# Reordering the steps of a bidirectional WKV kernel: r products two chunks ahead, an inverse ahead of a sigmoid, and a new order for a layer's first step

## The chip, the cores and the metric

The kernel runs on one core of a Trainium2 chip. The metric is device time in microseconds (us) of one execution, the median of three. Engines are named as the profile names them: PE is TensorE (matrix products), DVE is VectorE, ACT is ScalarE, POOL is GpSimd, SP is SyncE, which here only issues DMAs. Everything is in 32-bit floats.

## The reference

The input is `x`, 16 images of 192 channels and 56 x 56 = 3136 pixels. Three layers of the following kind are applied one after the other, and then one graph convolution. `_gn` is a group norm over 32 groups of channels.

```
# a WKV layer: x = x + layer(_gn(x)); t runs over the 3136 pixels
k, v, r = xs @ Wk.T, xs @ Wv.T, xs @ Wr.T
# forward: p, q are decayed sums of exp(k)*v and of exp(k)
y_t  = (p + e^(u+k_t) v_t) / (q + e^(u+k_t))      # then p, q take in pixel t
x_bi = 0.5 * (y of the pixels in order + y of the pixels in reverse)
h    = sigmoid(r) * x_bi
h    = (h - mean) * rsqrt(var + 1e-5)              # over the 192 channels
out  = h @ Wo.T
# the last layer: x + gelu(BN(concat(x, max of rolled differences) @ W + b))
```

## The kernel before

Two images make a pair, laid out as 128 partitions x 3 blocks x pixels (block 0: 128 channels of the first image, block 2: of the second, block 1: the remaining 64 of each). The 3136 pixels are cut into 7 chunks of 448. There are 8 pairs, and each goes through 3 WKV layers and the convolution; one pair in one layer is a *run*, so there are 32 runs. A WKV run has a forward pass over chunks 0 to 6 (functions `a_...`) and then a backward pass over chunks 6 to 0 (functions `b_...`). The sums are prefix scans on DVE (`scan`, L875).

Two streams of pairs are interleaved. While one run goes backward, a run of the other stream goes forward; I call these seven chunks a *turn*. The list of steps is worked out on the host in front of the launch. Turn by turn it has one backward chunk alone (`backward_alone`, chunk 6), then six steps in which a backward chunk and a forward chunk share the engines, then forward chunks alone. There are 24 turns. In 17 of them the forward run is a WKV run: their first shared step (backward chunk 5, forward chunk 0) is written in `both_a_first`, the five others (backward chunks 4 to 0) in `both_a`. In the other 7 the forward run is a convolution (`both_c`).

The order on each engine is written out by hand: the block runs under a manual schedule, so each engine executes its instructions in the order of the calls, and waits in that order. PE, DVE, ACT, POOL and SP each have a queue of their own. PSUM banks (7 of them) and SBUF slots (33) are handed out from lists in the order of the calls.

The work of one shared step, with the names used below:

- **r** (`b_gate`, L598 to L607): the product for the sigmoid, 14 matmuls. `b_exp` (L996) on ACT makes exp(-r) of it, `b_sigmoid` (L1003, L978) ln(1+...) and exp(-...).
- **k** and **v** (`a_keys`, `a_values`): the products of the forward chunk; `a_exp` (L920) on ACT, `a_ekv` (L940) on DVE.
- **scans** `b_q`, `b_p`, `a_q`, `a_p` (L875, DVE) and the **bonus** terms `b_den`, `b_num`, `a_den`, `a_num` (L890, DVE).
- **the inverses** of the denominators, on ACT as ln (L975) and exp(-...) (L978): of `b_den` for the mixing, of `a_den` for the forward output `a_y` (L982, POOL).
- **mixing** (`b_mix`, POOL, L1031, L1032, L1033 for each block): numerator x inverse, + forward output, x sigmoid.
- **the norm over channels**: `b_squares` (L1040, ACT); `b_sums` (L1047, L1049, PE) makes the sums **st**; `b_rs1` (L1055, ACT) squares the means; `b_rs2` (L1059, PE) subtracts them, called **rs2** below; `b_rs3` (L1063, L1065, ACT) makes the reciprocal deviation by ln and exp; `b_spread` (L1071, PE) spreads it over the partitions, **rsb**; `b_scale` (L1076, DVE) multiplies; `b_out` (PE, **ops**) is the product with Wo; `b_x` (L1089, DVE) adds it to x and stores x to DRAM.
- **count**: in a part of the steps ACT also takes two statistics (L734, L735) of a block of the next pair's input, twice per step.

In `both_a` the norm of a chunk is finished one step late: step *c* makes st of chunk *c* at its end, and rs2, rsb and ops of chunk *c* stand in the step after it. In `both_a_first` chunk 6's whole norm is done, and the sums of chunk 5.

`gap(...)` takes the next part of the coming run's group norm: sums, variance, `norm_fold` (POOL or DVE make the factor, L777 to L780, and ACT multiplies it into the weights of k and v, L770), and the weights of r.

On PE a `both_a` step has this order before: r of the next chunk, rs2, v, rsb, ops, k, st. On ACT: exp(-r), count, a save of the scan's edge, rs3, the sigmoid, the inverse for the mixing (blocks 0 and 2, then 1), the statistics of a stored chunk, squares and exps of k, rs1, and the inverse for y.

Of the kernel before, what the change touches and what calls it, by code (L numbers as in the profile page):

```python
# [55 lines left out]
NL = T // L  # L56
# [417 lines left out]
def fast_path(ctx: ExitStack, tc: tile.TileContext, flag, x, wproj, wfold, wcfold, wconst, wgroup, sums, picks, vecs, out):  # L474
# [499 lines left out]
    def ln(s, js=slice(0, 3)):  # L974
        S.activation(s.t[:, js, :], s.t[:, js, :], AF.Ln)  # L975
# [8 lines left out]


    def b_gate(run, c):
        product(run, "r", run.w[2], run.xb[c], c == NL - 1)

    def b_exp(run, c):
        if c == NL - 1:  # L990
# [328 lines left out]
    def count(z, most=1):  # L1319
        for _ in range(min(most, len(z))):  # L1320
            z_stats(*z.pop(0))

    def both_a(b, a, nback, nfront, z, loads):

        den = lambda: a[0].den[a[1]]
        l = of_stage(0.5)
        load_ahead(nback)
        store()
        if nback is not None:
            b_gate(*nback[1:])  # L1330
            b_exp(*nback[1:])
        count(z)
        b_q(*b)
        if l:
            b_rs2(*l)
            b_rs3(*l)
        b_sigmoid(*b)
        a_values(*a)
        if l:
            b_spread(*l)  # L1340
        b_p(*b)
        b_den(*b)
        for js in (AC, slice(1, 2)):
            ln(b[0].ek[b[1]], js)
            exp_minus(b[0].ek[b[1]], js)
        b_num(*b)
        b_mix(*b)
# [12 lines left out]
        b_squares(*b, (0,))  # L1360
        a_save(*a)
        count(z)
        exp_keys(nfront, (0, 2))
        b_squares(*b, (2,))
        exp_keys(nfront, (1,))
        b_squares(*b, (1,))
        b_sums(*b)
        a_p(*a)
        gap()
        a_den(*a)  # L1370
        b_rs1(*b)
        late[b] = 0.5
        invert(den())
        gap()
        a_num(*a)
        a_y(*a)
        gap()

    def both_a_first(b, a, nback, nfront, loads):

        den = lambda: a[0].den[a[1]]
        l = of_stage(0)
        load_ahead(nback)
        store()
        a_values(*a)
        b_squares(*l, (0, 2))
        b_q(*b)
        b_sigmoid(*b)
        b_p(*b)
        b_den(*b)  # L1390
        invert(b[0].ek[b[1]])
        b_num(*b)
        b_mix(*b)
        for u in loads:
            load_ahead(u)
        a_ekv(*a)
        b_squares(*l, (1,))
        if nback is not None:
            b_gate(*nback[1:])
        b_sums(*l)  # L1400
        b_rs1(*l)
        if nback is not None:
            b_exp(*nback[1:])
        a_q(*a)
        b_rs2(*l)
        b_rs3(*l)
        keys(nfront)
        a_p(*a)
        spread_and_scale(l)
        b_squares(*b, (0,))  # L1410
        a_save(*a)
        exp_keys(nfront)
        b_squares(*b, (2, 1))
        b_sums(*b)
        a_den(*a)
        b_rs1(*b)
        late[b] = 0.5
        invert(den())
        a_num(*a)
        add(l)  # L1420
        a_y(*a)

# [244 lines left out]
    def backward_alone(b, nback, nfront):  # L1667
        load_ahead(nback)
        load_ahead(nfront)
        store()  # L1670
        sum_up()
        b_q(*b)
        gap()
        b_den(*b)
        gap()
        invert(b[0].ek[b[1]])
        b_sigmoid(*b)
        b_p(*b)
        gap(G)
        b_num(*b)  # L1680
        b_mix(*b)
        for u in list(late):
            finish(u)
        if nback is not None:
            b_gate(*nback[1:])
            b_exp(*nback[1:])
        keys(nfront)
        exp_keys(nfront)
        late[b] = 0
# [13 lines left out]
    with tc.manual_schedule(engines={PE.engine, V.engine, S.engine, G.engine, nc.sync.engine}):  # L1703
        S.preload_act_table_set(TABLES)
        first = chains[0][0]
        for c in range(NL):
            load_ahead(("Z", first, c))
        for c in range(NL):
            count([(first, c, j) for j in ORDER], 3)
        for i, (b, f, z) in enumerate(steps):  # L1710
            nback, nfront, _ = steps[i + 1] if i + 1 < len(steps) else (None, None, None)
            for run in starts.get(i, ()):
                begin_later(run)
            if i == 0:
                keys(f)
                exp_keys(f)
            ahead = [("Z", run, c) for run, c, _ in (z if not b else [])]
            ahead += [nfront] if b and f else []
            ahead += [("Z", run, c) for run, c, _ in (steps[i + 1][2] if i + 1 < len(steps) else [])]
            ahead += [steps[i + 2][0]] if i + 2 < len(steps) else []  # L1720

            nkeys = nfront if nfront is not None and nfront[0] == "A" else None
            if f and not b and nkeys is None and nfront is not None and i + 2 < len(steps):
                far = steps[i + 2]
                if far[0] is None and far[1] is not None and far[1][0] == "A" and far[1][1] is f[1]:
                    nkeys = far[1]
            if f and nback is None and nfront is not None:
                near = [u for _, u, _ in steps[i + 1 : i + 4] if u is not None and u[0] == "A"]
                if len(near) > 1 and near[1][1] is near[0][1]:
                    ahead.append(near[1])  # L1730
            if not (b and f):
                for u in ahead:
                    load_ahead(u)
            if b and f and f[0] == "A":
                if of_stage(0) is None:
                    both_a(b[1:], f[1:], nback, nfront, z, ahead)
                else:
                    both_a_first(b[1:], f[1:], nback, nfront, ahead)
            elif b and f:
                both_c(b[1:], f[1:], nback, nfront, ahead)  # L1740
            elif f and f[0] == "A":
                forward_a(f[1:], nback, nfront, nkeys, z)
            elif f:
                forward_c(f[1:], nback, nfront)
            elif b:
                backward_alone(b[1:], nback, nfront)
            else:
                neither(nback, nfront)
            assert not z
        store()  # L1750
        assert not late and not unsummed and not convs and not half
# [100 lines left out]
```

## Time and profile before

| | us |
|---|---|
| median of 3 executions (lowest, highest) | 5217.34 (5207.30, 5221.48) |
| the profiled execution: its own time | 5220.16 |
| its span from first to last instruction | 5218.2 |
| PE busy | 4733.3 (91%) |
| DVE busy | 4750.5 (91%) |
| ACT busy | 3684.6 (71%) |
| POOL busy | 2889.2 (55%) |

A line of the profile names an engine, a line of the kernel, and output and inputs by the program's names. Times in timelines are us from the start of the span. PEclk is the share of its full clock that TensorE was granted. Busy time says how long an engine had something in hand; since two engines are at 91%, what matters is where each of them stands idle and for whom.

### The profile page before, as it was taken

Reading aid. Unit: us, or ns where it says so; the run is one execution under the profiler, and the core shown is the slowest. Engines: PE = TensorE matmul, PEld = TensorE weight load, DVE = VectorE, ACT = ScalarE, POOL = GpSimd, SP = SyncE. Lnnn points to the kernel's source line nnn. Section 1 sums busy time; section 2 is a strip of 40 time slices with the busy share of each in tenths; the row PEclk is TensorE's granted clock in tenths of the full one; section 3 lists DMA queues with packets and bytes.
Section 4 is the critical chain, followed back from the end, with each engine's and each line's share of the span. In section 5 each row is a group of like instructions: output and inputs, shape, how many; then the busy total and the mean of one; then the engine's idle time right before and its main releaser. Section 6 shows DMA issues by size and latency. Waiting matters only on the chain. (4 is left out here: it accounts for less than half of the span.)

```text
span 5218.2 us, 51856 instructions
## 1 busy us (share of the span) xinstructions
PE 4733.3 (91%) x15542; PEld 1498.8 (29%) x15542; DVE 4750.5 (91%) x6271; ACT 3684.6 (71%) x7163; POOL 2889.2 (55%) x2251
## 2 busy tenths in 40 slices
PE   7899998989899999998989999999898999999897
PEld 3222222223232222222323222222232322222222
DVE  6999999998989999999898999999889899999995
ACT  6777787776566777787656678777756667777772
POOL 1665665554545656565454556556545455666562
PEclk8999999999899999999989999999998999999998
DMA  5222222233232222223233223222333322222233
GB/s 154 69 82 87 90 86 89 85 110 97 90 116 72 87 90 93 82 90 122 93 93 101 84 75 100 88 85 87 128 93 101 93 74 77 72 84 77 80 104 120
DMA packets 314274, 482.47 MB, mean 92 GB/s; under 512 B 66432, under 2 KB 306688, under 8 KB 313984
## 3 DMA queue, kind: packets, MB, share of 16 engines
q1 hardware_dynamic: 312832, 477.59, 28.5%
q8 instruction: 126, 2.06, 0.2%
q10 hardware_dynamic: 1152, 1.48, 0.1%
q14 instruction: 164, 1.34, 0.1%
HBM read 324.83 MB, written 154.14 MB: 92 GB/s over the span
## 5 line engine op out<-in xcount | busy, mean ns | idle before, releaser
L875 DVE TENSOR_TENSOR_SCAN q<-fdecays,ek 128x449 f32<-128x449 f32 (+1 forms) x1008 | 1023.4, 1068 | 28.0 <-ACT ek L920 25.4
L875 DVE TENSOR_TENSOR_SCAN p<-fdecays,ekv 128x449 f32<-128x449 f32 (+1 forms) x1008 | 1020.3, 1065 | 0.6
L982 POOL TENSOR_TENSOR p<-p,q 128x1344 f32<-128x1344 f32 x168 | 512.0, 3047 | 830.3 <-ACT q L978 546.9
L1031 POOL TENSOR_TENSOR ekv<-ekv,ek 128x448 f32<-128x448 f32 x504 | 602.7, 1196 | 456.1 <-ACT ek L978 385.3
L1033 POOL TENSOR_TENSOR p<-p,sg 128x448 f32<-128x448 f32 x504 | 638.0, 1266 | 57.2 <-ACT ek L884 12.7
L1032 POOL TENSOR_TENSOR p<-p,ekv 128x448 f32<-128x448 f32 x504 | 606.1, 1203 | 39.5
L1040 ACT ACTIVATE ek<-p 128x448 f32<-128x448 f32 x504 | 286.4, 572 | 309.4 <-POOL p L1033 308.9
L886 POOL COPY ekv<-p 128x3 f32<-128x3 f32 x282 | 233.1, 827 | 488.0 <-DVE p L875 457.2
L1076 DVE TENSOR_TENSOR p<-p,rsb 128x448 f32<-128x448 f32 x504 | 282.4, 613 | 194.5 <-PE rsb L1071 194.4
L920 ACT ACTIVATE ek<-k,k 128x448 f32<-128x448 f32 x504 | 297.2, 632 | 225.3 <-PE k L601 179.2
L735 ACT ACTIVATE fjunk<-x 128x448 f32<-128x448 f32 x672 | 387.7, 577 | 40.1 <-DVE x L1089 13.4
L1071 PE MATMUL rsb<-rs,fpicks 32*128 32x448 f32 (+1 forms) x1008 | 359.2, 629 | 42.4 <-ACT rs L1065 42.4
L1159 POOL TENSOR_TENSOR ml<-ml,x 128x1344 f32<-128x1344 f32 x56 | 178.9, 3194 | 391.8 <-ACT ml L1150 391.8
L890 DVE SCALAR_TENSOR_TENSOR ek<-ek,fcc,q 128x896 f32<-128x896 f32 x336 | 379.1, 1167 | 0.0
L890 DVE SCALAR_TENSOR_TENSOR q<-ek,fcc,q 128x896 f32<-128x896 f32 x336 | 359.2, 1109 | 6.3 <-ACT cvb L954 4.6
L1089 DVE SCALAR_TENSOR_TENSOR x<-ops,fwob,x 128x448 f32<-128x448 f32 x504 | 314.2, 670 | 46.7 <-PE ops L601 26.6
L734 ACT ACTIVATE fjunk<-x 128x448 f32<-128x448 f32 x600 | 342.5, 571 | 11.4
L996 ACT ACTIVATE sg<-r,r 128x448 f32<-128x448 f32 x504 | 313.0, 627 | 33.5 <-PE r L607 20.7
L890 DVE SCALAR_TENSOR_TENSOR ekv<-ekv,fcc,p 128x896 f32<-128x896 f32 x336 | 330.1, 1022 | 0.0
L940 DVE SCALAR_TENSOR_TENSOR ekv<-v,v,ek 128x448 f32<-128x448 f32 x504 | 312.5, 672 | 16.6 <-PE v L601 8.0
L975 ACT ACTIVATE q<-q 128x1344 f32<-128x1344 f32 x168 | 221.5, 1318 | 125.5 <-DVE q L890 101.3
L890 DVE SCALAR_TENSOR_TENSOR p<-ekv,fcc,p 128x896 f32<-128x896 f32 x336 | 295.3, 919 | 6.5 <-POOL ekv L886 1.7
(235 smaller groups left out, 11546.4 us busy)
## 6 DMA issues: line engine op xcount, KB each, us to landing
x<-xd SPq DMA_DIRECT2D x240, 672.0 KB, 5.3
xd<-x SPq DMA_DIRECT2D x168, 672.0 KB, 3.9
x<-in_x_dram SPq DMA_DIRECT2D x320, 224.0 KB, 4.3
x<-in_x_dram SPq DMA_DIRECT2D x320, 112.0 KB, 4.2
out_dram<-ml SPq DMA_DIRECT2D x112, 224.0 KB, 2.3
m<-xd SPq DMA_DIRECT2D x112, 168.0 KB, 5.1
wkv<-in_wfold_dram SPq DMA_DIRECT2D x24, 640.0 KB, 5.6
out_dram<-ml SPq DMA_DIRECT2D x112, 112.0 KB, 2.3
```

The lines of the kernel that those rows point to most:

```text
L734: S.activation(junk, xt[:, j, :], AF.Identity, accum_out=stats[:, 0, j, c : c + 1])
L735: S.activation(junk, xt[:, j, :], AF.Square, accum_out=stats[:, 1, j, c : c + 1])
L875: V.tensor_tensor_scan(out, dec[:, column(j)].to_broadcast([P, L if first else L + 1]), e, 0.0, ALU.mult, ALU.add)
L890: by_channel(lambda js, i: V.scalar_tensor_tensor(dst.t[:, js, :], e.t[:, js, :], cc[:, i : i + 1], state.t[:, js, :], ALU.mult, ALU.add))
L940: V.scalar_tensor_tensor(e.t[:, j, :], ps[j][:, 0:L], b[:, j, :], run.ek[c].t[:, j, :], ALU.add, ALU.mult)
L982: G.tensor_mul(run.h[c].t, run.h[c].t, den.t)
L996: S.activation(sg.t[:, j, :], ps[j][:, 0:L], AF.Exp, bias=b[:, j, :], scale=-1.0, accum_out=run.chk[:, at : at + 1])
L1031: G.tensor_mul(y.t[:, j, :], y.t[:, j, :], den.t[:, j, :])
L1032: G.tensor_add(h.t[:, j, :], h.t[:, j, :], y.t[:, j, :])
L1033: G.tensor_mul(h.t[:, j, :], h.t[:, j, :], sg.t[:, j, :])
L1071: PE.matmul(ps[j][:, :L], pick[rows, j, :], rs[rows, :], start=True, stop=True)
L1089: V.scalar_tensor_tensor(xj, ps[j][:, 0:L], wob[:, column(j)], xj, ALU.add, ALU.add, accum_out=run.new[:, 0, j, c : c + 1] if c == 0 else ...
```

## The change

Five things are moved; nothing is computed in another way.

1. In `both_a`, r is made two chunks ahead: the product for backward chunk *c*-2 stands in step *c*, between the last squares and the sums. The call at the start of a step is kept, and `once` makes it do nothing where r was made before. So step 4 makes r of chunks 3 and 2, step 3 that of 1, step 2 that of 0, and steps 1 and 0 none.
2. In `both_a`, v stands ahead of rs2, and rs3 ahead of the count. PE's order becomes v, rs2, rsb, ops, k, r, st.
3. In `both_a`, the inverse for y stands ahead of rs1 on ACT; the inverse for the mixing's blocks 0 and 2 stands ahead of the sigmoid, that of block 1 behind it.
4. In `both_a_first`, the forward scan of q, the save and the product with exp(k) stand ahead of the backward bonus; chunk 6's rsb and ops stand ahead of k; the sigmoid stays ahead of the inverse, chunk 6's rs1 stands behind that inverse, and the inverse for y is taken ahead of the squares of chunk 5.
5. In `backward_alone`, the part of the next run's norm stands ahead of the sigmoid and of `b_p`.

```diff
     def b_gate(run, c):
-        product(run, "r", run.w[2], run.xb[c], c == NL - 1)
+        if once(run, "r", c):
+            product(run, "r", run.w[2], run.xb[c], c == NL - 1)
...
     def both_a(b, a, nback, nfront, z, loads, far):
         if nback is not None:
             b_gate(*nback[1:])
             b_exp(*nback[1:])
-        count(z)
-        b_q(*b)
+        a_values(*a)
         if l:
             b_rs2(*l)
             b_rs3(*l)
-        b_sigmoid(*b)
-        a_values(*a)
+        count(z)
+        b_q(*b)
         if l:
             b_spread(*l)
         b_p(*b)
         b_den(*b)
-        for js in (AC, slice(1, 2)):
-            ln(b[0].ek[b[1]], js)
-            exp_minus(b[0].ek[b[1]], js)
+        ln(b[0].ek[b[1]], AC)
+        exp_minus(b[0].ek[b[1]], AC)
+        b_sigmoid(*b)
+        ln(b[0].ek[b[1]], slice(1, 2))
+        exp_minus(b[0].ek[b[1]], slice(1, 2))
...
         b_squares(*b, (1,))
+        if far:
+            b_gate(*far[1:])
         b_sums(*b)
         a_p(*a)
         gap()
         a_den(*a)
+        invert(den())
         b_rs1(*b)
         late[b] = 0.5
-        invert(den())
...
     def both_a_first(b, a, nback, nfront, loads):
         b_p(*b)
+        a_q(*a)
+        a_save(*a)
+        a_ekv(*a)
+        b_squares(*l, (1,))
         b_den(*b)
         invert(b[0].ek[b[1]])
         b_num(*b)
         b_mix(*b)
...
-        a_ekv(*a)
-        b_squares(*l, (1,))
         if nback is not None:
             b_gate(*nback[1:])
         b_sums(*l)
         b_rs1(*l)
+        b_rs2(*l)
+        b_rs3(*l)
         if nback is not None:
             b_exp(*nback[1:])
-        a_q(*a)
-        b_rs2(*l)
-        b_rs3(*l)
+        a_p(*a)
+        a_den(*a)
+        invert(den())
+        spread_and_scale(l)
         keys(nfront)
-        a_p(*a)
-        spread_and_scale(l)
         b_squares(*b, (0,))
-        a_save(*a)
         exp_keys(nfront)
         b_squares(*b, (2, 1))
         b_sums(*b)
-        a_den(*a)
+        a_num(*a)
         b_rs1(*b)
         late[b] = 0.5
-        invert(den())
-        a_num(*a)
...
     def backward_alone(b, nback, nfront):
         invert(b[0].ek[b[1]])
+        gap(G)
         b_sigmoid(*b)
         b_p(*b)
-        gap(G)
...
+            far = steps[i + 2][0] if nback is not None and i + 2 < len(steps) else None
+            if far is not None and far[1] is not nback[1]:
+                far = None
```

More of the change, by code (lines that the diff above doesn't have):

```diff
@@ L1321, in count, with both_a @@
             z_stats(*z.pop(0))
-    def both_a(b, a, nback, nfront, z, loads):
+    def both_a(b, a, nback, nfront, z, loads, far):
         den = lambda: a[0].den[a[1]]
@@ L1723, in fast_path @@
             if f and not b and nkeys is None and nfront is not None and i + 2 < len(steps):
-                far = steps[i + 2]
-                if far[0] is None and far[1] is not None and far[1][0] == "A" and far[1][1] is f[1]:
-                    nkeys = far[1]
+                then = steps[i + 2]
+                if then[0] is None and then[1] is not None and then[1][0] == "A" and then[1][1] is f[1]:
+                    nkeys = then[1]
             if f and nback is None and nfront is not None:
@@ L1733, in fast_path @@
                     load_ahead(u)
+            far = steps[i + 2][0] if nback is not None and i + 2 < len(steps) else None
+            if far is not None and far[1] is not nback[1]:
+                far = None
             if b and f and f[0] == "A":
                 if of_stage(0) is None:
-                    both_a(b[1:], f[1:], nback, nfront, z, ahead)
+                    both_a(b[1:], f[1:], nback, nfront, z, ahead, far)
                 else:
```

## The prediction

> **What bounds the kernel now.** First the page's busy times, which name two engines at once:
>
> ```profile
> PE 4733.3 (91%) x15542; PEld 1498.8 (29%) x15542; DVE 4750.5 (91%) x6271; ACT 3684.6 (71%) x7163; POOL 2889.2 (55%) x2251
> ```
>
> So an average decides nothing, and I cut windows one `both_a` step long: two of a turn without counts, two of a turn with them (columns: stretch, length, then busy time of PE, its weight loads, DVE, ACT, POOL, and the granted clock).
>
> ```profile
> 409.10:432.70 23.60, 23.26 (x80) 7.12 (x80) 23.60 (x30) 19.25 (x38) 15.32 (x12) 1.00 0.28 89
> 432.70:456.20 23.50, 23.26 (x80) 7.12 (x80) 23.50 (x30) 19.24 (x37) 15.29 (x12) 1.00 0.26 87
> 1888.40:1915.50 27.10, 25.03 (x80) 7.64 (x80) 25.00 (x30) 21.58 (x45) 15.65 (x13) 0.94 0.22 76
> 1915.50:1942.70 27.20, 25.13 (x80) 7.65 (x80) 25.00 (x30) 21.59 (x45) 15.65 (x13) 0.94 0.30 97
> ```
>
> Without counts the step is 23.56 us and DVE never rests; PE lacks 0.3 us. With counts it is 27.2 us, nobody is full, and the clock falls below 1. Going through the starts of rsb turn by turn, 8 of the 17 turns are of the first kind, 9 of the second; three intervals of each turn (rsb of chunk 5 to 4, 3, 2) hold an r and are meant below.
>
> The waits say what the counted step hangs on:
>
> ```profile
> PEld st L1049 <- POOL p L1033: 191.9, 90, 4.1
> PE st L1049 <- POOL p L1033: 119.7, 90, 3.3
> ```
>
> PE idles 2.09 us for the mixing's end; then a half-clock spell; then r, exp(-r), the count, rs3, the sigmoid and the inverse stand in one row on ACT before POOL can mix again.
>
> The third reading is what surrounds rs2 on PE. In a counted step now, and then in a place where rs2 is followed at once by rsb:
>
> ```profile
> 1895.87 0.96 PE L1059 MATMUL st<-rs,fpicks 64*64 64x448 f32 x2
> 1896.76 1.02 PE L598 MATMUL v<-x,wkv 128*128 128x448 f32 x2
> ...
> 1901.27 1.97 PE L1071 MATMUL rsb<-rs,fpicks 32*128 32x448 f32 x6
> ```
>
> ```profile
> 1531.25 0.96 PE L1059 MATMUL st<-rs,fpicks 64*64 64x448 f32 x2
> 1533.54 3.55 PE L1071 MATMUL rsb<-rs,fpicks 32*128 32x448 f32 x6 [1.32 <-ACT rs L1065]
> 1537.01 1.86 PE L598 MATMUL v<-x,wkv 128*128 128x448 f32 x2
> ```
>
> ```profile
> 1530.30:1533.70 3.40, 2.08 (x9) 0.55 (x10) 3.40 (x10) 2.39 (x5) 0.53 (x1) 1.00 0.88 307
> 1533.70:1537.10 3.40, 3.40 (x7) 0.82 (x7) 3.33 (x6) 3.24 (x11) 0.00 (x0) 0.50 0.83 263
> 1537.10:1540.50 3.40, 3.40 (x6) 1.29 (x8) 3.40 (x6) 0.58 (x2) 0.00 (x0) 0.50 0.12 38
> 1540.50:1543.90 3.40, 3.40 (x12) 1.17 (x13) 3.12 (x4) 0.21 (x1) 0.00 (x0) 1.00 0.00 0
> ```
>
> Where v lies between them, ACT's ln and exp of rs3 (0.63 + 0.57 us) are hidden. Where it does not, PE idles 1.32 us and the clock then falls to half: rsb takes 3.55 instead of 1.97. This kernel has 23 places with a full product, rs2, 1.32 us and rsb at full clock, and all 23 are followed by a half-clock spell within 3.1 us. In 17 of the 23 the spell lasts 6.83 us, in the other six 3.41; in six of the 17 PE had a product ready right behind rsb.
>
> **What the Trainium skill says.** "TensorE: Matmul & The Clock Gate", Part 1: the clock goes to half or full by PE's activity in free-running windows of about 3.4 us. The trace agrees (spells of 3.41 or 6.83 us at 0.50), but the page warns of idle gaps above about 3.4 us, and here 1.32 us is enough: rs2 and rsb fill only part of the array. The measurement decides. The same page, Part 2, says that PE pulls only weight loads ahead, while matmuls keep their order; so nothing behind rsb can fill that gap. "SBUF — State Buffer", Who interferes with whom: a DVE instruction with two SBUF inputs and a GpSimd one that reads SBUF lock each other out. The trace agrees: bonus L890 on q takes 2.59 us instead of 1.71 where it meets mixing, and L1033 2.05 instead of 1.15.
>
> **The change, part by part.** Durations on PE, start to start: a product 4.51, st 1.64, rs2 0.89, rsb 1.90. Sums are made against the span, 5218.2; the profiled execution took 5220.2, 0.05% above the median of 5217.3.
>
> *`both_a`, v ahead of rs2, r ahead of st.* PE's loop becomes v, rs2, gap, rsb, ops, k, r, st = 4 x 4.51 + 0.89 + 1.90 + 1.64 = 22.5, with the gap (1.32, and 0.07 of lost overlap) 23.9; I take 24.05, since 23.57 minus the 0.31 idle and the 0.6 of slow st, plus 1.39, gives that. What else could bind, from rs2's end: ACT has rs3 1.25, count 1.33, save 0.2, inverse of two blocks 1.9, sigmoid 2.65, inverse of block 1 1.15, statistics 4.2, then 5.0 of squares, exps, save and count, which puts the last square's end at 17.7; half of st, v and rs2 behind it end at 24.0, as PE's own loop does. ACT's total, 21.6, has room, and the 2.65 of the inverse for y now ahead of rs1 is covered by v. DVE needs 23.55, with counts and some 1.3 us of locking 24.8. r's input: SP issued the load at 1874.26, it landed at 1878.79, and PE reaches r about 1885; r's banks come free with the x addition 8.2 us behind `b_scale`, about 10.6 on this scale, r starts at 12.3. So both are hidden, by 6 and 1.7 us. SP's own order of loads and stores is the same in both kernels.
>
> The gap throttles. By the window's phase I take no spell in 0.1 of the steps, one window (half of 3.41 = 1.7 lost) in 0.25, two (3.4) in 0.65: 2.6 us. The trace bounds this from 0 to 3.4, at six of its places two windows despite a ready product. Interval: 24.05 + 2.6 = 26.65. Against 27.2 with counts: -0.55 x 27 = -15. Against 23.56 without: +3.1 x 24 = +74. The interval from chunk 2 to 1 and the last one hold no r; DVE sets them (19.8 + 25.2 to 26.5, or 24.8 + 20.8 to 21.1: both 45 to 46), DVE's order there is unchanged: 0. The mixing's inverse ahead of the sigmoid starts POOL up to 2.65 earlier in the counted step; this is inside the loop, since PE ends it.
>
> *`both_a_first` and `backward_alone`, on PE from r of chunk 5 (511.5 in the turn at 500) to rsb of chunk 5 (553.5).* Now PE idles there 2.75 (k waits for L770) and 0.65. The fold ahead of the sigmoid takes away 2.7, since POOL's factor can be ready at 509.9 and ACT's inverse ends at 510.9. Added: (a) rs1 of chunk 6 now stands behind the inverse of chunk 5. On DVE `b_q`, `b_p` end at 518.8, `a_q` 521.8, exp(k)v 523.9, `b_den` 525.5; inverse to 528.2, rs1 528.7; PE ended st at 526.75: 2.0 idle in place of 0.65. (b) rs2 directly ahead of rsb: 1.3. (c) k now comes last, so st of chunk 5 waits for exp of k's block 1 and two squares behind it: 1.2. (d) rs2, gap, rsb in the first `both_a`: 1.3. Sum -2.7 + 1.35 + 1.3 + 1.2 + 1.3 = +2.4; a and c could be nothing and a shorter wait elsewhere could take 0.5 more: from 0 to 3. The two gaps of (a) and (b) throttle too: +2.6 (0 to 3.4; the gap of (d) is counted with the interval behind it). 5.0 x 17 = +85. Locking of `b_den` with chunk 6's mixing (3.15 instead of 1.72) goes, but DVE then only waits for rsb.
>
> *Convolution turns.* Only `backward_alone` acts: mixing of chunk 6 begins 2 us sooner; DVE waits 1.0 us for its end in L1125. -1.0 x 7 = -7 (0 to -14).
>
> Sum: -15 + 74 + 85 - 7 = +137, 5355; I state 5350.
>
> **The rivals.**
>
> *One window per gap* (spells end as soon as ops runs): loss 1.7, interval 25.75: -1.45 x 27 + 2.19 x 24 + 4.1 x 17 - 7 = +76, 5294. For it: six of the 23 spells last 3.41. Against: these begin a full us after rsb's end, and the six with a product ready all lasted 6.83.
>
> *Faster: no throttling.* r in PE's idle time keeps each window busy enough. Then DVE sets the counted step, 24.8: -2.4 x 27; without counts +0.5 x 24; first steps +2.4 x 17; -7: -19, 5199; with (a) and (c) absent and PE's 24.05 in counted steps too, about 5135. It decides at a loss of 0.28 us per gap: there 68 gaps (51 and 17) cost those 19. Against it stand 23 of 23 places; for it, r now runs right up to st.
>
> *r gets stuck*: its load or its bank late by more than the margins above; PE, with st and v behind r, stalls, above 5400. SP's longest waits are for stores, which are later than these loads; unlikely.
>
> **How the numbers follow.** Main case 0.50 (5310 to 5385), one window 0.25, no throttling 0.20, stuck 0.05. What a measurement can tell from no change is 0.3%, 16 us. Faster: 0.19, of the no-throttle case nearly all; same: 0.06, from the lower edge of the one-window case; slower: 0.75. The range reaches from the no-throttle case's 5195 to 5390.
>
> **What would show it.** Right: L1071 waiting for L1065 some 1.3 us in about 68 more places; mean granted clock below the 0.935 of before; steps without counts at 25.7 to 27.4 and DVE idle ahead of L1076; the wait of L1049 for POOL nearly gone; k no longer waiting for L770. Wrong: clock at 1.00 through `both_a`, steps of 24 to 25 us in both kinds of turn, or rsb of chunk 6 to chunk 5 far from 24 to 27 us (17.95 now).

## The result, and the profile after

The changed kernel takes 5394.9 us (median; 5391.63 to 5406.7), the kernel before beside it 5212.32 us. The ratio is 1.0356, with a 95% interval of 1.0327 to 1.0385: 3.6% slower. I had forecast 5350 and a range up to 5390. The side and the main mechanism, the gap between rs2 and rsb, were right; the time lies 5 us above the range, so the size was not. The profiled execution took 5391.6, its span 5389.7; before it was 5218.2, so 171.5 us have to be found.

The first part of the page, busy times, after:

```profile
PE 4857.8 (90%) x15542; PEld 1540.9 (29%) x15542; DVE 4694.5 (87%) x6271; ACT 3663.7 (68%) x7163; POOL 2854.1 (53%) x2251
```

The instructions are the same in number. PE alone is busier, by 124.5 us, with the same matmuls: it ran them at a lower clock (granted 0.905, was 0.935). Four windows one `both_a` step long, after: two of a turn with counts, then two of a turn without (stretch, length, busy PE, weight loads, DVE, ACT, POOL, granted clock, DMA).

```profile
588.80:615.90 27.10, 25.78 (x82) 7.97 (x82) 24.52 (x29) 21.37 (x46) 18.60 (x15) 0.87 0.31 103
615.90:643.00 27.10, 25.78 (x82) 7.99 (x82) 24.52 (x29) 21.37 (x46) 15.28 (x12) 0.87 0.23 81
1723.60:1749.10 25.50, 24.18 (x82) 7.63 (x82) 24.31 (x29) 19.02 (x38) 15.27 (x12) 0.93 0.25 82
1749.10:1776.20 27.10, 25.78 (x82) 7.99 (x82) 23.77 (x29) 18.91 (x38) 15.30 (x12) 0.87 0.23 76
```

Both kinds of turn now have the same step: PE ends it, DVE no longer fills the step without counts, and the clock is 0.87 or 0.93. The one wait that makes it, in the timeline of PE at the start of the last of these steps:

```profile
1746.77 0.96 PE L1060 MATMUL st<-rs,fpicks 64*64 64x448 f32 x2
1749.06 3.20 PE L1072 MATMUL rsb<-rs,fpicks 32*128 32x448 f32 x6 [1.32 <-ACT rs L1066]
1752.19 1.86 PE L598 MATMUL ops<-p,fwo 128*128 128x448 f32 x2
1753.85 1.70 PE L599 MATMUL ops<-p,fwo 128*128 128x448 f32 x2
```

rs2, 1.32 us of idle, rsb: behind it rsb takes 3.20 instead of 1.97, and the first matmuls of ops 1.86 and 1.70 instead of 1.02 and 0.91. The waits after (engine and line, what it waited for, us in total, times, longest):

```profile
PE rsb L1072 <- ACT rs L1066: 177.4, 134, 1.3
...
PEld st L1050 <- POOL p L1034: 40.4, 17, 4.4
...
PE st L1050 <- POOL p L1034: 28.1, 13, 3.6
```

The same wait of rsb was 42.4 us in 32 places before, and st waited for POOL 119.7 us in 90 places. So the wait that bounded the counted step went as meant, 92 us of it, and another took its place.

Sorted by stage, from the starts of rsb and the ends of r in both timelines (a first step is the stretch from the end of r of chunk 5 to rsb of chunk 5; an interval is from the rsb of one chunk to the next):

| stage | forecast, us | measured, us |
|---|---|---|
| 27 intervals of `both_a` with counts (chunk 5 to 2) | -15 | -22.8 |
| 24 intervals without counts | +74 | +55.7 |
| 8 first steps, turns without counts | 8 x 5.0 = +40 | +52.5 |
| 9 first steps, turns with counts | 9 x 5.0 = +45 | **+104.3** |
| rsb of chunk 2 to 0, 17 turns | 0 | +18.8 |
| rsb of chunk 0 to the end of the next turn's r of chunk 5, 17 turns | 0 | -19.0 |
| 7 turns with a convolution | -7 | -16.9 |
| ahead of the first turn | 0 | -1.0 |
| sum | +137 | +171.6 |

The fourth row, with the third, is where the forecast broke: together 72 us over. ACT's timeline in a first step with counts, after:

```profile
552.31 0.52 ACT L1056 ACTIVATE rs<-st 64x448 f32<-64x448 f32 x1
553.88 0.63 ACT L1064 ACTIVATE rs<-st,feps 64x448 f32<-64x448 f32 x1 [1.05 <-PE st L1060]
554.54 0.57 ACT L1066 ACTIVATE rs<-rs 64x448 f32<-64x448 f32 x1
562.98 0.64 ACT L997 ACTIVATE sg<-r,r 128x448 f32<-128x448 f32 x1 [7.86 <-POOL p L1033]
```

and PE's in the same stretch:

```profile
552.88 0.96 PE L1060 MATMUL st<-rs,fpicks 64*64 64x448 f32 x2 [0.93 <-ACT rs L1056]
555.17 3.72 PE L1072 MATMUL rsb<-rs,fpicks 32*128 32x448 f32 x6 [1.32 <-ACT rs L1066]
558.82 1.86 PE L598 MATMUL ops<-p,fwo 128*128 128x448 f32 x2
564.37 1.86 PE L599 MATMUL ops<-p,fwo 128*128 128x448 f32 x2 [3.69 <-ACT sg L997]
```

exp(-r) of the next chunk (L997) waits 7.86 us for POOL's mixing (L1033). It reads r, which PE had finished at 550.3; what it lacks is a place for its output. By the call that gives slots back, the SBUF slot handed to it is the one of the numerator, which mixing still reads at L1033; in six of the nine turns it waits longer, 9.07 us, for L1034, behind which the slot of the sigmoid comes free. The PSUM banks of r therefore stay full, and ops, in the middle of its product, waits 3.69 us for one of them; the inverse for y, k and st stand behind. Over the nine turns that wait is

```profile
PE ops L599 <- ACT sg L997: 40.5, 9, 4.9
```

In a first step without counts the same exp(-r) starts right behind rs3, at 4745.44 after a rs3 that began at 4744.84.

### The profile page after: what moved, and what is told of

The parts are those of the page before. It is cut to its first block, busy times and chain, and to the rows that moved or that the text cites. A ratio compares the mean times of both kernels' runs of the same rounds, so it can differ in the third digit from the quotient of the medians.

```text
span 5389.7 us, 51972 instructions
## 1 busy us (share of the span) xinstructions
PE 4857.8 (90%) x15542; PEld 1540.9 (29%) x15542; DVE 4694.5 (87%) x6271; ACT 3663.7 (68%) x7163; POOL 2854.1 (53%) x2251
## 3 DMA queue, kind: packets, MB, share of 16 engines
q14 instruction: 165, 1.35, 0.1%
## 5 line engine op out<-in xcount | busy, mean ns | idle before, releaser
L875 DVE TENSOR_TENSOR_SCAN p<-fdecays,ekv 128x449 f32<-128x449 f32 (+1 forms) x1008 | 1022.1, 1069 | 23.9 <-PE st L1050 23.0
L1034 POOL TENSOR_TENSOR p<-p,sg 128x448 f32<-128x448 f32 x504 | 613.3, 1217 | 75.6 <-ACT sg L978 32.9
L1033 POOL TENSOR_TENSOR p<-p,ekv 128x448 f32<-128x448 f32 x504 | 595.5, 1182 | 39.5
L1072 PE MATMUL rsb<-rs,fpicks 32*128 32x448 f32 (+1 forms) x1008 | 437.2, 730 | 177.4 <-ACT rs L1066 177.4
L997 ACT ACTIVATE sg<-r,r 128x448 f32<-128x448 f32 x504 | 312.6, 628 | 125.8 <-POOL p L1034 54.4
L1064 ACT ACTIVATE rs<-st,feps 64x448 f32<-64x448 f32 x168 | 105.7, 629 | 384.2 <-PE st L1060 384.2
L890 DVE SCALAR_TENSOR_TENSOR ek<-ek,fcc,q 128x896 f32<-128x896 f32 x336 | 333.2, 1033 | 0.0
```

What stands on the lines that cost most here:

```text
L875: V.tensor_tensor_scan(out, dec[:, column(j)].to_broadcast([P, L if first else L + 1]), e, 0.0, ALU.mult, ALU.add)
L890: by_channel(lambda js, i: V.scalar_tensor_tensor(dst.t[:, js, :], e.t[:, js, :], cc[:, i : i + 1], state.t[:, js, :], ALU.mult, ALU.add))
L997: S.activation(sg.t[:, j, :], ps[j][:, 0:L], AF.Exp, bias=b[:, j, :], scale=-1.0, accum_out=run.chk[:, at : at + 1])
L1033: G.tensor_add(h.t[:, j, :], h.t[:, j, :], y.t[:, j, :])
L1034: G.tensor_mul(h.t[:, j, :], h.t[:, j, :], sg.t[:, j, :])
L1072: PE.matmul(ps[j][:, :L], pick[rows, j, :], rs[rows, :], start=True, stop=True)
```

## The experiments

Ratios are to the kernel before in the same group of runs (5199.7 to 5221 us, by group). The experiments move calls or change when a slot is taken; those with a filler add products that are not used for anything.

**The slot.** `e1_sg_slot`: the changed kernel, but the slot is taken at the start of `both_a_first`.

```
@@ both_a_first
         load_ahead(nback)
+        if nback is not None:
+            slot_of(nback[1].sg, nback[2], "sg")
@@ b_exp
-        sg = run.sg[c] = Slot("sg")
+        sg = slot_of(run.sg, c, "sg")
```

> The changed kernel, but in both_a_first the SBUF slot for exp(-r) of the next chunk is taken from the list at the start of the step, ahead of everything else. Slot theory: in the 9 turns with counts exp(-r) waits 7.9 us for the mixing (L1033), because it was handed the slot of a numerator that the mixing still reads; without that the stretch from rsb of chunk 6 to that of chunk 5 goes from 33.7 to 35.8 us to about 28.3, as in the turns without counts: some 6 us in 9 turns, about -55 us against the changed kernel, ratio to before about 1.022 to 1.026. Rival: ACT is merely early there and another wait follows in its place (the mixing itself ends late): less than 15 us, ratio above 1.032.

Measured: 1.0271 (1.0242 to 1.0301), 0.0085 or some 44 us less than the change as made. First steps with counts fell from +11.6 to +7.1 us a turn, those without counts stayed (+6.6, now +7.7). The timeline of ACT in such a first step:

```profile
948.77 0.57 ACT L1066 ACTIVATE rs<-rs 64x448 f32<-64x448 f32 x1
949.37 0.64 ACT L997 ACTIVATE sg<-r,r 128x448 f32<-128x448 f32 x1
```

exp(-r) follows rs3 at once. The slot theory holds; it accounts for the difference between the two kinds of turn. The half-clock time in the first steps with counts fell with it, from 15.9 to 9.9 us on average.

**The clock.** `e2_fill`: the changed kernel, with one 128x128x448 product between rs2 and rsb in `both_a`, into the bank that rsb then overwrites.

```
     def b_spread(run, c, fill=False):
         ps = run.ps["rsb"] = banks("rsb")
+        if fill:
+            PE.matmul(ps[0][:, :L], gmat[:, 0:P], gmat[:, 0:L], start=True, stop=True)
```

> The changed kernel with one more 128x128x448 product in both_a between rs2 and rsb, on PE only, of constants, written to a bank that rsb overwrites; it depends on nothing that rs3 makes, takes about 0.9 us and so fits in the 1.32 us gap. Clock theory: the gap costs little itself; the half-clock spell behind it costs 1.7 to 3.4 us. Filled, most spells in both_a go: the intervals of 25.5 and 27.1 us become 23.9 to 24.8, some 2 us in each of about 85 steps that have one, -90 to -150 us against the changed kernel, ratio about 1.007 to 1.018, mean clock above 0.93. Gap theory (the order itself, ACT's wait and the mixing make the 27.1): no change or 0.5 us more per step, ratio 1.035 or above.

Measured: 1.0183 (1.0166 to 1.0200), granted clock 0.933. PE does more and the kernel is 1.7% faster, some 90 us. The place of before, now:

```profile
1717.95 0.96 PE L1060 MATMUL st<-rs,fpicks 64*64 64x448 f32 x2
1718.85 1.02 PE L1072 MATMUL rsb<-fgmat 128*128 128x448 f32 x2
1720.24 1.97 PE L1074 MATMUL rsb<-rs,fpicks 32*128 32x448 f32 x6 [0.38 <-ACT rs L1066]
1722.34 0.64 PE L598 MATMUL ops<-p,fwo 128*128 128x448 f32 x1
```

rsb starts as late as with the idle gap (2.29 us behind rs2), but it takes 1.97 again. The intervals show it best (all 51 that hold an r, as counts of rounded lengths):

| kernel | 27 with counts, mean | 24 without, mean | values |
|---|---|---|---|
| before | 27.19 | 23.56 | 26.9 to 27.3; 23.5 and 23.6 |
| changed | 26.35 | 25.88 | 23.9 to 24.4 (10), 25.5 to 26.0 (11), 26.8 to 27.1 (30) |
| changed, filler | 24.80 | 24.12 | 23.8 to 24.4 (40), 25.5 to 26.0 (4), 27.0 to 27.1 (7) |

By the clock of the trace, the intervals of the second row hold no window at half clock (10 of them, 23.91 us on average), one (14, 25.85) or two (27, 27.10); half of one window of 3.41 us is 1.7. The forecast for the three was 24.05, 25.75 and 27.45. With the filler 42 of the 51 intervals hold none, and 9 hold one.

**The first step.** `e3_first_before`: the changed kernel with `both_a_first` as before.

> The changed kernel with both_a_first in its old order; both_a and backward_alone stay changed. If the loss sits mainly in the first step, as the stretches from r of chunk 5 to rsb of chunk 5 say (+6.6 us in 8 turns, +11.6 in 9, 157 us in all, with 1.3 us of gap and the spell behind it belonging to both_a), most of it goes: -110 to -150 us, ratio about 1.006 to 1.014. If both_a's own gap and clock carry it, less than 60 us go, ratio above 1.023.

Measured: 1.0058 (1.0035 to 1.0080), some 155 us less than the change. Of the loss, then, more than four fifths hung on the new order of the seventeen first steps. The difference to `e1_sg_slot`, where the slot no longer waits, is 0.0213 or 111 us: 6.5 us for each first step (7.6 by the stretches of the two traces). Both kernels have the changed `backward_alone` and the gap (d) of the prediction, so this is to be held against its other terms, 1.35 + 1.3 + 1.2 + 2.6 = 6.45, and not against 5.0. The order without the slot was priced about right; the slot comes on top.

`e10_mended`: the change with the slot as above and the filler in `both_a` and `both_a_first`.

> The whole change, with both of its faults taken out as far as they can be: the SBUF slot for exp(-r) taken at the start of both_a_first (worth 44 us alone), and one 128x128x448 filler product between rs2 and rsb in both_a (worth 98 us alone) and now also in both_a_first. The filler computes nothing that is used. If the slot wait and the half-clock spells are the whole loss, and the first step's two gaps cost 2.6 us in each of 17 turns: 5395 - 44 - 98 - 44 = about 5210, ratio 0.996 to 1.003. If the first step's order itself costs more than its forecast 2.4 us, or its spells stay: 1.006 to 1.012.

Measured: 1.0111 (1.0094 to 1.0127): the hope for 0.996 to 1.003 missed, and the other reading, that the first step costs more or keeps its spells, held. First steps still cost +7.9 without and +7.5 with counts. The timeline of PE in one:

```profile
4610.91 1.75 PE L1060 MATMUL st<-rs,fpicks 64*64 64x448 f32 x2 [2.30 <-ACT rs L1056]
4612.59 1.86 PE L1072 MATMUL rsb<-fgmat 128*128 128x448 f32 x2
4614.38 3.65 PE L1074 MATMUL rsb<-rs,fpicks 32*128 32x448 f32 x6
```

rs2 itself already runs at half clock (1.75 instead of 0.96): the spell comes from the wait ahead of rs2, where PE stands 2.3 us for rs1 behind ACT's inverse. Here the filler behind it ran at half clock too. The half-clock time in the first steps was 11.5 us without and 10.2 with counts, no less than in `e1_sg_slot` (11.5 and 9.9). So the next run filled that wait.

```
@@ both_a_first
+        ps = b_fill(l[0])      # four filler products into rsb's bank
         b_rs2(*l)
```

> As the mended whole change, and in both_a_first also four filler products (used for nothing, about 1.7 us) between the sums of chunk 6 and rs2, where TensorE waits 2.3 to 3.5 us for the squares of the means, which stand behind an inverse on ScalarE. In the mended kernel a half-clock spell of 10.2 us began with that rs2 in the steps looked at. Theory: this wait is what lowers the clock in the first step; the spells there go, 3.4 to 5.1 us in each of 17 turns come back, 58 to 87 us: ratio 0.995 to 1.000. Rival: what the first step still loses is the waits themselves and what is late behind them: no gain, 1.008 to 1.013, or slower where a filler product has to wait for its bank.

Measured: 1.0002 (0.9989 to 1.0016), the upper edge of what I expected and clear of the rival. The same place:

```profile
4584.07 3.27 PE L1071 MATMUL rsb<-fgmat 128*128 128x448 f32 x8
4587.27 0.96 PE L1060 MATMUL st<-rs,fpicks 64*64 64x448 f32 x2
4588.17 1.02 PE L1078 MATMUL rsb<-fgmat 128*128 128x448 f32 x2
4589.56 2.04 PE L1080 MATMUL rsb<-rs,fpicks 32*128 32x448 f32 x6 [0.37 <-ACT rs L1066]
```

rs2 and rsb run at full clock, although the four products took 3.2 us, more than the 1.7 I had said and 0.5 to 1 us more than the wait they fill. Half-clock time in the first steps fell to 2.6 and 0.4 us, and they now cost +5.0 and +4.7. With the slot and the clock mended the change is worth nothing: it equals the kernel before.

**The other parts one at a time.** `e4_back_alone`: the kernel before with `gap(G)` ahead of the sigmoid in `backward_alone`, part 5 of the change.

> The kernel before with the changed backward_alone alone (the fold of the next run's weights ahead of the sigmoid). My prediction's step: k of the first step starts 2.7 us sooner in 15 turns where PE waits for it, and mixing 1 us sooner in the 7 convolution turns: -25 to -50 us, ratio 0.990 to 0.995. Rival: what k gains is given back before the next turn, since the sigmoid and exp(-r) are 1.7 us later on ACT: ratio 0.997 to 1.003.

Measured: 0.9920 (0.9903 to 0.9936), 44 us faster. In the profile the stretch from the end of r of chunk 5 to rsb of chunk 6 shrank by 6.4 us over the eight turns without counts, 14.1 over the nine with counts and 6.5 over the seven with a convolution, 27 together. The prediction had credited the seventeen with 2.7 each, 46 us, and they gave 20.5: four of them had no wait for L770 to lose, and where k does start 2.8 us sooner, st then waits for ACT's squares (L1040), and rs2 starts only 1.4 us sooner. The convolution turns were another 24 us shorter further on; but so they were (22 to 23) in `e5_r_ahead` and `e8_inverse_first`, where nothing in them is changed, so this is not shown to be the edit's.

`e5_r_ahead`: the kernel before with r two chunks ahead, part 1 alone; v stays behind rs2.

> The kernel before with r made two chunks ahead, between k and st in both_a, and nothing else: v stays behind rs2. Theory (v's place makes the loss, r's place gains): r covers PE's 2.09 us wait for the mixing in the steps with counts; the row from the mixing's end to its next start is then st 0.9, rs1 0.5, inverse for y 2.7, exp(-r) 2.1, count 1.3, rs3 1.3, sigmoid 2.7, inverse 1.9 and mixing 11.6, 25.0 us instead of 27.2: -2.2 x 27 = -60 us; steps without counts stay at 23.6, DVE-bound: ratio 0.986 to 0.991. Rival: r two ahead itself hurts (it holds three banks longer, or comes in st's way): ratio 1.00 or above.

Measured: 1.0072 (1.0054 to 1.0091): slower, a miss. Intervals without counts went from 23.6 to 25.5, those with counts only from 27.2 to 26.2. Windows of two steps without counts:

```profile
4655.40:4680.80 25.40, 22.68 (x82) 7.09 (x82) 25.40 (x30) 19.04 (x38) 15.24 (x13) 1.00 0.25 83
4680.80:4707.80 27.00, 24.29 (x82) 7.62 (x82) 27.00 (x30) 19.01 (x38) 15.18 (x13) 0.94 0.15 52
```

DVE is full in both, with the same 30 instructions as before, in 25.4 and 27.0 us instead of 23.6. One of them has grown; DVE's timeline, and POOL's at the same place:

```profile
4679.62 2.60 DVE L890 SCALAR_TENSOR_TENSOR ek<-ek,fcc,q 128x896 f32<-128x896 f32 x2
...
4704.99 4.25 DVE L890 SCALAR_TENSOR_TENSOR ek<-ek,fcc,q 128x896 f32<-128x896 f32 x2
```

```profile
4677.63 3.05 POOL L982 TENSOR_TENSOR p<-p,q 128x1344 f32<-128x1344 f32 x1 [6.06 <-ACT q L978]
...
4704.65 3.04 POOL L982 TENSOR_TENSOR p<-p,q 128x1344 f32<-128x1344 f32 x1 [7.71 <-ACT q L978]
```

The bonus `b_den` takes 1.72 us where nothing disturbs it and 4.25 where it runs beside POOL's product for y. "SBUF — State Buffer", Who interferes with whom, in the Trainium skill, says that two such instructions lock each other out; the case agrees, and here it costs up to 2.5 us at once. In the turns without counts `b_den` of chunks 3, 2 and 1 took 3.68 us on average, 1.71 before; the difference is all that the intervals grew by (1.97). Why do they meet now? As I read the order, r stands ahead of st on PE, so st and rs1 come a product later; on ACT the inverse for y stands behind rs1; so POOL has its product later, and `b_den` has come.

`e6_v_behind`: the change without its new first step, with v behind rs2 and rs1 ahead of the inverse for y, both as before. `e7_rs3_first`: that, with rs3 ahead of exp(-r).

> The changed kernel with both_a_first as before, v behind rs2 again, and rs1 ahead of the inverse for y; r two ahead, the split inverse ahead of the sigmoid, the count behind rs3 and backward_alone stay changed. Theory: without rs2 directly ahead of rsb there is no gap and no spell in both_a; steps with counts come to 23.6 to 25 us (DVE), those without stay at 23.6: -60 to -85 us, and some -40 from backward_alone: ratio 0.975 to 0.983. Rival: the half-clock spells come from the whole order and not from v's place: above 0.995.

> As the one with v behind rs2, and in addition rs3 ahead of exp(-r) on ACT, so that rsb's input is ready 2.1 us sooner. Theory: v's 4.5 us and rs2's 0.9 on PE against rs1 0.5, inverse 2.7, exp(-r) 2.1, rs3 1.3 on ACT, 6.5 us: rsb is some 0.5 us late without this, on time with it: 0 to 0.6 us in 68 steps, 0 to -40 us against the other, ratio 0.970 to 0.983. Rival: DVE sets the step in both; no difference.

Measured: 0.9925 (0.9905 to 0.9945) and 0.9948 (0.9931 to 0.9965). The first expectation missed, and so did its rival: no more came of it than `backward_alone` gave by itself. In the second the rival held: rs3 earlier gave nothing. Intervals are 25.3 in both kinds of turn, DVE is busy for 24.9 of them, and `b_den` of chunks 3, 2 and 1 takes 3.4 to 3.8 us on average. I had left the inverse for y behind rs1, which keeps the collision. So the next kernel is `e6_v_behind` with one call moved.

```
@@ both_a
+        invert(den())
         b_rs1(*b)
         late[b] = 0.5
-        invert(den())
```

> As the kernel with v behind rs2 and the first step as before (0.9925), but with the inverse for y ahead of rs1 in both_a, as the change has it. What makes r two chunks ahead dear there: DVE is busy 24.9 of 25.3 us in its intervals, and the backward bonus of q takes 3.4 us there instead of 1.8 before, where it meets GpSimd's product for y, which comes later because the inverse for y stands behind rs1 and rs1 behind r. Theory of the collision: with the inverse ahead of rs1 the product for y is early again, the bonus is back at 1.8, intervals 23.6 to 24.1; ratio 0.974 to 0.982. Rival, the bare latency: rs2 has nothing before it now that hides rs1, TensorE waits there and the clock falls, whatever the bonus takes: intervals stay at 25 or above, ratio 0.990 or more.

Measured: 0.9707 (0.9691 to 0.9723), 5064 us, the fastest of all, and below the range that the collision theory gave. Two steps without counts and two with:

```profile
4485.00:4508.50 23.50, 22.60 (x84) 7.09 (x82) 23.50 (x30) 19.16 (x38) 15.34 (x12) 1.00 0.28 89
4508.50:4532.00 23.50, 22.52 (x82) 7.05 (x80) 23.50 (x31) 19.18 (x38) 15.35 (x12) 1.00 0.18 59
1816.50:1840.00 23.50, 22.61 (x82) 7.09 (x80) 23.50 (x30) 21.41 (x46) 15.35 (x12) 1.00 0.28 96
1840.00:1863.60 23.60, 22.62 (x84) 7.11 (x82) 23.60 (x31) 21.49 (x46) 15.37 (x12) 1.00 0.33 110
```

All four are alike: DVE full, PE with 0.9 us to spare, the clock at 1.00. POOL's product for y is over before `b_den` begins:

```profile
4502.21 3.03 POOL L982 TENSOR_TENSOR p<-p,q 128x1344 f32<-128x1344 f32 x1 [3.47 <-ACT q L978]
```

```profile
4506.79 1.72 DVE L890 SCALAR_TENSOR_TENSOR ek<-ek,fcc,q 128x896 f32<-128x896 f32 x2
```

The rival, the bare latency, falls with PE's timeline:

```profile
4501.86 0.55 PE L1050 MATMUL st<-ek,fsums 128*32 128x448 f32 x2
4503.06 0.96 PE L1060 MATMUL st<-rs,fpicks 64*64 64x448 f32 x2 [0.66 <-ACT rs L1056]
4503.96 1.02 PE L598 MATMUL v<-x,wkv 128*128 128x448 f32 x2
```

PE does wait for rs1, 0.66 us, in all 51 of these intervals, and none of them has a half-clock spell. PE has that time, and the gap is harmless there.

This kernel differs from `e3_first_before` by one line: v behind rs2 and rs3 instead of ahead of them. That line moves the ratio from 1.0058 to 0.9707, 183 us, and the intervals from 26.2 to 23.4. It is the plainest measurement of what the gap between rs2 and rsb costs with the spell behind it.

`e8_inverse_first`: the kernel before, with the mixing's inverse of blocks 0 and 2 ahead of the sigmoid in `both_a`; part of 3 alone.

```
-        b_sigmoid(*b)
         a_values(*a)
...
-        for js in (AC, slice(1, 2)):
-            ln(b[0].ek[b[1]], js)
-            exp_minus(b[0].ek[b[1]], js)
+        ln(b[0].ek[b[1]], AC)
+        exp_minus(b[0].ek[b[1]], AC)
+        b_sigmoid(*b)
+        ln(b[0].ek[b[1]], slice(1, 2))
+        exp_minus(b[0].ek[b[1]], slice(1, 2))
```

> The kernel before with the mixing's inverse of blocks 0 and 2 ahead of the sigmoid in both_a, and nothing else. Theory: in the steps with counts the sigmoid's 2.65 us leave the row that leads to the mixing, so its end, st and r come up to 2.65 us sooner: up to -2.4 us in 27 intervals, -40 to -65 us, ratio 0.987 to 0.992; without counts the inverse then waits for b_den on DVE, nothing. Rival: ACT waits for b_den there too and the sigmoid only moves behind that wait: ratio 0.997 to 1.003.

Measured: 0.9764 (0.9747 to 0.9781), 126 us faster than before and more than twice what I expected. The 27 intervals with counts account for 96 us of it: 27.19 to 23.64 on average, about as short as those without (23.49). Windows of two such steps:

```profile
757.30:781.80 24.50, 23.67 (x82) 7.12 (x80) 24.50 (x31) 22.27 (x47) 15.39 (x12) 1.00 0.37 122
781.80:804.80 23.00, 23.00 (x84) 7.24 (x82) 22.79 (x30) 19.41 (x41) 15.40 (x12) 1.00 0.27 84
```

PE or DVE is full in each, and the clock is 1.00 (0.94 before). The waits of st for POOL:

```profile
PEld st L1049 <- POOL p L1033: 57.2, 42, 4.4
...
PE st L1049 <- POOL p L1033: 24.3, 9, 3.6
```

90 waits became 9. The idle before st was 2.09 us, and each of the 27 intervals held one window at half clock (1.7 us lost); with one exchange on ACT none of them does, and most of the idle is gone. DVE also got back 0.87 us in each of these intervals, since the forward bonus on q no longer meets the end of mixing (1.72 us, was 2.59).

`e9_both_good`: this and the changed `backward_alone` together. `e11_fill_tail`: that with a filler in `finish`.

> The kernel before with two parts of the change: the mixing's inverse ahead of the sigmoid in both_a, and the changed backward_alone; r, v, rs1 and both_a_first stay as before. Parts add: the inverse alone gave 0.976 (97 us of it in the steps with counts); backward_alone took about 37 us in its trace outside the convolution turns' later steps, and those were 24 us shorter in other kernels too. Theory: 5095 less 25 to 37, about 5060 to 5070, ratio 0.968 to 0.972. Rival: what backward_alone gave was the same time as the inverse gave (no gain on top): 0.976. Steps with and without counts both near 23.6 us.

> As the kernel with both good parts, and one filler product (used for nothing) between rs2 and rsb where a chunk is finished at the end of a turn, which is where the kernel before has its 1.32 us gaps, each followed by a half-clock spell. Theory: the spells behind those places go; where PE sets the pace there, up to 1.7 to 3.4 us in each of 17 turns: half-clock time down by some 100 us, and 10 to 40 us faster, ratio 0.960 to 0.969. Rival: DVE and ACT set the pace at a turn's end, the spells cost nothing: equal to the kernel with both good parts, at 0.968 to 0.972.

Measured: 0.9762 (0.9746 to 0.9778) and the same 0.9762. The first is the rival's value: `backward_alone` adds nothing to the inverse that the ratios can tell. The rival's reason, that both gained the same time, is not what the traces show: the first steps of `e9_both_good` are 30 us shorter than those of `e8_inverse_first`, and its convolution turns 11 us longer. Whether the two parts add stays open. At 5077 us it too is faster than the kernel before and the changed one. The second tells nothing on the filler: `finish` isn't where those gaps are, the filler ran in one place only, and the run repeats the one before it. Whether the half-clock spells at a turn's end cost anything was not tried.

## Why the prediction was right and wrong

**What bounds the kernel**: right. The counted step hung on POOL's mixing through the row on ACT; `e8_inverse_first` shows it, by taking the sigmoid's two instructions out of that row.

**The gap throttles**: right, in mechanism and nearly in size. I had put intervals at 26.65; they are 26.35 and 25.88. The distribution was a little too pessimistic: no window, one and two with chances of 0.1, 0.25 and 0.65, against 10, 14 and 27 of 51. `e2_fill` shows the cause by filling the gap, and `e13_y_ahead` beside `e3_first_before` by closing it. The rival with one window per gap falls with the 27 intervals that hold two, though its mean, 25.75, is close to the 25.88; the faster one without throttling falls too: its turning point was a loss of 0.28 us per gap, and the gaps lost 2.0 to 2.4 on average (25.88 and 26.35 less the 23.9 of steps without a spell).

**`both_a_first` and `backward_alone`, "5.0 x 17 = +85"**: this is the step that failed. It measured +6.6 in the turns without counts and +11.6 in those with, together +157. From the starts on PE, term by term, us for each first step:

| term | forecast | 8 turns without counts | 9 with counts |
|---|---|---|---|
| k no longer waits for L770 (up to the start of st) | -2.7 | -1.5 | -3.0 |
| (a) rs2 waits for rs1, beyond the 0.65 of before | +1.35 | +0.9 | +0.7 |
| (b) rs2 directly ahead of rsb | +1.3 | +1.4 | +1.4 |
| (c) st of chunk 5 waits | +1.2 | +1.2 | +1.2 |
| (d) the same gap in the first `both_a` | +1.3 | +1.4 | +1.4 |
| throttling (rsb and ops slower) | +2.6 | +3.0 | +5.4 |
| ops waits for a bank of r | 0 | +0.1 | +4.5 |
| sum | +5.0 | +6.6 | +11.6 |

Two terms make the excess of 72 us. The last was put at nothing and cost 41 us, and `e1_sg_slot` shows its cause: a slot of SBUF. For r I had priced a late load and a late bank (the rival "r gets stuck"), each with a margin, but not the slot of what exp(-r) writes. The edit put the forward save and the product with exp(k) ahead of the backward bonus; as I read the calls, one more slot is then taken before exp(-r) asks for one, and in counted turns, where the next pair's chunks lie in slots as well, the next one in the list is mixing's. The second is the throttling, 28 us more than its 2.6: I had let (a) and (b) share at most two half-clock windows, 6.8 us, and the traces show 9.4 us at half clock in a first step without counts and 15.9 in one with. A part of that is the slot's doing, since the wait of ops prolongs the spell (9.9 us in `e1_sg_slot`). The rest, about 4 us a step as `e10_mended` runs it, goes when the wait (a) is filled (`e12_fill_first`); I had blamed both (a) and (b) for the spell, and with (b) filled (a) alone is enough.

The wait of (a) measured 1.88 us in four of the turns without counts, where I had 2.0, but 1.3 on average in the others. The credit for k was read off one turn: ten of the 17 turns had a wait of 2.75 to 3.06 us for L770, three one of 1.41, and four none. These two errors, -9 and +7 us, nearly cancel. With the slot mended the kernel takes 5346 us, 4 from the 5350 that I stated. That is luck: in its trace the first steps are still 40 us over the forecast, and the convolution turns 34 under it.

**The tail from chunk 2 to 0, "0"**: wrong by +18.8. I counted about 68 new places where rsb waits for rs3 and there are 102, six in each of 17 turns: the two intervals without an r have the gap too, and lose 0.55 us each. Half-clock time in the pair rose from 6.2 to 12.1 us, but most of that slowing costs nothing there, which would fit that DVE sets these intervals.

**The mixing's inverse, "inside the loop, since PE ends it"**: this fits the change as a whole (no run takes the exchange out of it), and it hid from me what the part is worth alone. In the changed kernel PE's gaps end the step; in the kernel before the exchange buys 96 us in the counted steps. Likewise r two chunks ahead and the inverse for y ahead of rs1 were priced as one row with v. Taken apart, r alone costs 0.7%, by a collision that the inverse for y mends, and with it mended r seems to gain: `e13_y_ahead` at 0.9707 lies below `e9_both_good` at 0.9762. Besides r and the inverse for y these two differ in the place of the count, so how much of this is r's is not shown. That rs2 would have to wait for rs1 I had not considered; it was harmless.

**Convolution turns, "-7"**: `e4_back_alone` shows -6.5 at the place named. In the changed kernel that place gave -2.9, and the other 14 us are of the kind that also appears where nothing in these turns was altered (two kernels that do the same there, `e9_both_good` and `e11_fill_tail`, differ by 11 us in them); their cause is open. Part of it belongs to the trace of before: its convolution turns behind rsb of chunk 6 take 1716.7 us in all, more than in any of the other 14 traces (1688 to 1707).

On the clock, the Trainium skill has a closer passage than the one I used: "TensorE: Matmul & The Clock Gate", Part 1, A second HAM failure mode, tells of another kernel in which short idle stretches between groups of matmuls, if frequent, also made the clock swing. This case agrees and puts numbers to it: one gap of 1.32 us beside rs2 and rsb in each step lost the clock in 41 of 51 steps, and with one filler product of 0.8 us in it 42 of 51 steps kept it.

## What to carry to other kernels

Before a product is moved on an in-order engine, write down which latency of another engine it covers on each side; one of them will be bare afterwards, and where the bare gap lies decides what it costs: between rs2 and rsb 183 us, ahead of rs2 nothing that the traces show. Where an instruction is moved, ask also what it writes to (slots and banks handed out in the order of calls change hands) and what its followers will now run beside. And price the parts of a change alone: the whole loses 3.6%, while without two of its parts, v's place and the first step, it wins 2.9%.

## What was new on the hardware

- With more work on PE the kernel got faster: one product of 0.8 us in each `both_a` gap gave back some 90 us, and four in the first step's wait took 1.0111 to 1.0002, 57 us.
- The idle needed to lose the clock was small where narrow matmuls stand beside it: 1.32 us between rs2 (64x64) and rsb (32x128), in all 23 places of before that the prediction lists and in 41 of 51 steps of the changed kernel. A gap of 0.66 us between st and rs2 never did, in 51 of 51 intervals of `e13_y_ahead`. And in the kernel before PE idles longer between two whole products, r and k, in the first step:

```profile
514.28 1.02 PE L598 MATMUL k<-x,wkv 128*128 128x449 f32 x2 [2.75 <-ACT wkv L770]
```

  In none of the seven turns with a gap of 2.75 us there did a half-clock spell follow, nor in 12 of 15 such places of `e5_r_ahead` and `e8_inverse_first`; behind the three gaps of 3.06 us of the kernel before it did. That the width of the neighbours makes the difference is not shown by itself: no run changed the width alone.
- Where the filler stood mattered. Behind a 2.3 us wait, in `e10_mended`, rs2 itself ran at 0.5 (1.75 us instead of 0.96), and the filler product behind it took 1.79 us; put into the wait, in `e12_fill_first`, four products kept rs2 and rsb at full clock.
- Two instructions of DVE took 2.5 times as long beside one of GpSimd: 4.25 us instead of 1.72 for the two bonus terms of `b_den` beside the 3.04 us product for y. A reordering on PE brought them together, and no wait shows it: DVE looks merely busy (25.40 of 25.40 us, 27.00 of 27.00).
